# Storing the stream in token order from a ScalarE copy beside layer two, reading it without a step in the scan layer, and a gate product placed behind the eighth scan

## The chip, the core and the metric

The kernel runs on one core of one Trainium2 chip, as one launch. The metric is the device time of that launch in microseconds (us). The kernel before the change took 3594.66 us as the median of 3 runs (3594.13 to 3596.95). Five engines work on one program: PE multiplies matrices into PSUM, DVE and ACT work on vectors, POOL is the general engine, and SP issues most of the transfers. Each has an instruction stream of its own, and they meet at semaphores.

## What is computed

An input of three images, 256 channels, 48 x 48 pixels, runs through four layers, each of which adds its result to the stream and begins with a group norm over 32 groups:

```python
x = x + L0(gn(x))    # 1x1 convolutions, two blocks of attention across the images, MLPs
x = x + L1(gn(x))    # 3x3 convolution whose weights are mixed from 8 experts per image
x = x + L2(gn(x))    # 3x3 convolution
x = x + L3(gn(x))    # a selective scan (Mamba) over the 2304 pixels of each image
...
# L3, for tokens l in order, d of 512 inner channels, n of 16 states:
xn = layernorm(x); x_in, z = split(xn @ in_proj)
u  = silu(causal_conv4(x_in)); dt_raw, B, C = split(u @ x_proj)
dt = softplus(dt_raw @ dt_proj + bias)
h[l] = exp(dt[l] * A) * h[l-1] + dt[l] * B[l] * u[l]
y[l] = sum_n h[l] * C[l] + u[l] * D
out  = (y * silu(z)) @ out_proj
```

Everything is float32. The change touches the end of L2 and all of L3.

## The kernel before, in words

**The stream and its order.** Between the layers the stream of an image lies in SBUF as `xs[b]`, 128 partitions x 2 groups of channels (`ct`) x 2304 pixels. The pixels are in phase order: pixel column modulo 4 is the outer index `j`, so that a Winograd transform of the 3x3 convolutions reads and writes packed rows. The scan layer needs the pixels as tokens one after the other.

**Layers one and two** are one loop over `halves` (L1442): six units (two layers x images 2, 1, 0, the tuple `ORDER`), each in an upper and a lower half `h`. For each half, `input_transform` (L295) of the *next* half is emitted first: ACT writes the normalised pixels, padded, into the one buffer `xpad`, and twelve DVE operations make `vt` from it (`L329` and `L334` are the last that read `xpad`, in one or the other order). Then `output` (L1364) runs twice, for m = 0 and 1: six groups of six matmuls each (`products`, L1352) go to one of five PSUM banks `ps_c`; ACT copies every second one to `cb` (L1372), and DVE adds sums and differences to `xs[b]`; the last two go straight from PSUM to `xs[b]` (L1386). After a unit, `next_norm` (L1413) takes the moments of the finished image with two ACT passes over it (`moments`, L1393, which writes its waste into `xpad`). In layer two, after the lower half, six DMAs per image store `xs[b]` to the DRAM tensor `xd[b]` (L1460), chunk by chunk, with the phases still outermost within a chunk: runs of 96 elements. SP issues them, ACT those of the last image.

**Preparation beside layer two.** The generator `early_preparation` (L1272) is advanced after each group of `products` from unit 4 on: it loads chunks 0 and 1 of the stream, normalises them and does the scan layer's projections for chunk 0. A scheduler in the layer below decides the final order of instructions of each engine in this stretch from estimated times; in the attention and in the scan layer the order is the one written out (`keep_order`, L1660).

**The scan layer** goes over 18 chunks of 384 tokens (six per image). A chunk has 8 steps (m of 4 groups of inner channels, h of 2 groups of states). A step is eight scans on DVE (`scan`, L1569), each fed by a decay that ACT computes into one of three PSUM slots (`decay`, L1556), so that ACT can be three ahead. Then DVE and POOL fill the next step's buffer (`fill`, L1529), POOL multiplies the states by C (`times_c`, L1576), and PE sums over the states into `ps_y` (`add_states`, L1585, of the step before). `gate` (L1602) multiplies the finished sum of a group m by silu(z); it is called in the second step of the next group, after scan 6 (`part == 5`, L1625), and it frees the single `ps_y` bank for the next group's first product, D times u (L1592). Three lists of stages (`plan`, `after`, `gating`, L1217 to L1264) place the preparation of the next chunks and the output of the last one into the steps; the place MID is after scans 2 and 6, LATE after 4 and 8, PE_ on PE's stream. Among them:

- `group_scale` (L1053): reads the loaded chunk `xp`, applies the group norm and writes it to `xg` in token order, a step of four elements on the write side; then `less_mean`, `centre`, `square_mean`, `inverse_root`, `normalise` and `tokens` make the layer norm.
- `silu` (L1122): a table load, a Silu over 1536 elements, a table load back, once for u (after m = 1, h = 1) and once for z (after m = 0, h = 0).
- `residual` (L1204) loads the chunk again into `ot`; `project_y` (L1196) multiplies by out_proj and adds the residual with a matmul by the identity (L1202), which reads `ot` through `in_order` (L1049): every step along the tokens is 96 elements. `store` (L1208) copies to `ot` and sends it out.
- `spread` (L1497) loads `dtr` and `dtur`, dt and dt times u, from DRAM for each m. SP's DMAs take turns on eight semaphores, and a DMA waits for the one that used its semaphore before.

Of the kernel before, what the change touches and what calls it, by code (L numbers as in the profile page):

```python
# [9 lines left out]
F32 = mybir.dt.float32  # L10
I32 = mybir.dt.int32
AF = mybir.ActivationFunctionType
# [4 lines left out]
P = 128  # L17
B = 3
HW = 48
N = HW * HW  # L20
CT = 2
# [4 lines left out]
CH = 384  # L26
NCH = N // CH
# [56 lines left out]
def net(  # L84
# [66 lines left out]

    ycat = [dram.tile([P, 3, N], F32, name=f"ycat{b}", bufs=1) for b in range(B)]

    xd = [dram.tile([P, NCH, CT, CH], F32, name=f"xd{b}", bufs=1) for b in range(B)]
    norm3 = {}

    def rsqrt_eps(var, n):
# [67 lines left out]
    def exp_ln_tables():  # L225

        nc.scalar.preload_act_table_set("natural_log_exp_and_others")
# [715 lines left out]


    psg = ctx.enter_context(tc.tile_pool(name="psg", bufs=1, space=PSUM))
    rooms, w3v, chunks = {}, {}, {}

    def room(k, name):
        return rooms[name][k.at % len(rooms[name])]
# [15 lines left out]
    def w3_rooms():  # L965

        block = upools[0].tile([P, 6, 3, CT, 256], F32, name="u")
        block = block.rearrange("p a b c d -> p (a b c d)")
        w3v.update(divide(
            block, ("w3sb", P, (NW3,)), ("wtap", P, (DCONV, CT, DI * P)), ("dtsb", DTR + 1, (DI * P,)),  # L970
            ("amat", P, (DI * DS,)), ("rep", P, (4, 32)), ("less", P, (2, P)), ("zero", P, (8,)),
            ("xn0", P, (CT, CH + DCONV - 1)), ("xn1", P, (CT, CH + DCONV - 1)),
        ))
        rooms["xn"] = [w3v["xn0"], w3v["xn1"]]
        pieces = [wst.tile([P, 3 * 256], F32, name="wconv") for _ in range(6)]
        halves = [t.rearrange("p (t n) -> p t n", t=2) for t in pieces]
        for name, got in zip(("xp", "xg", "sq", "ot"), (halves[:1], halves[1:2], halves[2:3], halves[3:5])):
            rooms[name] = got
        rooms["dbc"] = [halves[5][:96, j, :] for j in range(2)]

# [52 lines left out]
    def fetch(at):  # L1033
        k = chunks[at] = Chunk()
        k.at = at
        k.b, k.c = todo[at]
        k.before = chunks.get(at - 1)
        k.xp = room(k, "xp")
        nc.sync.dma_start(k.xp, xd[k.b][:, k.c])

    class Chunk:
        pass
# [3 lines left out]

    def in_order(t):  # L1049

        return t.rearrange("p (j n) -> p n j", j=4)

    def group_scale(k):  # L1053
        sc, sh = norm3[k.b]
        k.xg = room(k, "xg")
        for ct in range(CT):
            nc.scalar.activation(
                k.xg[:, ct, :].rearrange("p (n j) -> p j n", j=4),
                k.xp[:, ct, :].rearrange("p (j n) -> p j n", j=4), AF.Identity,
                bias=sh[:, ct : ct + 1], scale=sc[:, ct : ct + 1],  # L1060
            )

# [133 lines left out]
    def project_y(k, mo):  # L1196
        for m in range(DI):
            nc.tensor.matmul(  # L1198
                bank[mo], w("out", m * 256 + mo * P, P), k.sz[:, m, :],
                start=m == 0, stop=False,  # L1200
            )
        nc.tensor.matmul(bank[mo], ident, in_order(k.ot[:, mo, :]), start=False, stop=True)  # L1202

    def residual(k):  # L1204
        k.ot = room(k, "ot")
        nc.sync.dma_start(k.ot, xd[k.b][:, k.c])

    def store(k, mo):  # L1208
        nc.scalar.copy(k.ot[:, mo, :], bank[mo])  # L1209
# [56 lines left out]
    def run(at, j, place):  # L1266
        for when, where, rel, stage in after + plan + gating:
            if (when, where) == (j, place) and 0 <= at + rel < len(todo):
                stage(chunks[at + rel])


    def early_preparation():  # L1272

        exp_ln_tables()
        fetch(0)
        winx, cwb = x2_rooms()
        k = chunks[0]
        yield
        while 2 not in norm3:
            yield  # L1280
        group_scale(k)
        yield
        for tap in (0, 1):
            fold_taps(winx, cwb, tap)
        less_mean(k)
        yield
        centre(k)
        yield
        square_mean(k)
        yield  # L1290
        for tap in (2, 3):
            fold_taps(winx, cwb, tap)
        inverse_root(k)
        yield
        normalise(k)
        tokens(k)
        fetch(1)
        yield
        for m in (0, 1):
            taps(k, m, 0, 4)  # L1300
            yield
        take_u(k, 0)
        take_u(k, 1)
        yield
        for m in (2, 3):
            taps(k, m, 0, 4)
            yield
        take_u(k, 2)
        take_u(k, 3)
        silu(k.u)  # L1310
        yield
        k = chunks[1]
        for stage in (group_scale, less_mean, centre, square_mean, inverse_root, normalise):
            stage(k)
            yield
        tokens(k)
        yield

        k = chunks[0]
        while 1 not in norm3:  # L1320
            yield
        x1_rooms()
        yield
        project_u(k)
        yield
        take_dbc(k)
        yield
        for m in (0, 2):
            project_dt(k, m)
            yield  # L1330
            softplus(k, m)
            yield
            take_dt(k, m)
            yield
            keep_dt(k, m)
            yield
        for m in (0, 2):
            for j in range(2):
                project_z(k, m + j, j)
            yield  # L1340
            for j in range(2):
                take_z(k, m + j, j)
            yield


    with ExitStack() as l1:
# [88 lines left out]
        def between():  # L1435
            next(pending, None)
            if at_unit >= 4:
                next(early, None)

        vt = first_v  # L1440
        pending = iter(())
        for n, (k, h) in enumerate(halves):  # L1442
            layer, b = units[k]
            at_unit = k
            if k == 3 and h == 0:
                w3_rooms()
                w3_loads()
            ahead = transformed(n + 1) if n + 1 < len(halves) else None
            u = weights[B if layer else b]
            for m in range(2):  # L1450
                output(b, h, m, u, vt, v("l2_bias", 0, 2) if layer else None)
                for _ in range(13):
                    next(beside.get(k, iter(())), None)
            vt = ahead
            if layer and h == 1:
                phases = xs[b].rearrange("p t (j n) -> p (t j) n", j=4)

                queue = nc.sync if k + 1 < len(units) else nc.scalar
                for c in range(NCH):
                    queue.dma_start(  # L1460
                        xd[b][:, c].rearrange("p t (j n) -> p (t j) n", j=4),
                        phases[:, :, c * (CH // 4) : (c + 1) * (CH // 4)],
                    )
            if h == 1:
                for _ in pending:
                    pass
                pending = next_norm(layer, b)
                next(pending)
        for _ in pending:
            pass  # L1470
        for _ in early:
# [8 lines left out]
    with ExitStack() as l3:  # L1480
# [121 lines left out]
        def gate(at, m):  # L1602
            k = chunks[at]
            nc.vector.tensor_tensor(k.sz[:, m, :], k.y_ps[:, :CH], k.sz[:, m, :], ALU.mult)
# [10 lines left out]
        for s, (at, m, h) in enumerate(steps):  # L1615
            if m == 0 and h == 1 and at + 2 <= last:
                fetch(at + 2)
            for part in range(8):
                j = 4 * m + 2 * h + part // 4
                scan(s, part)  # L1620
                decay(8 * s + part + 3)
                if part == 4 and s + 1 < len(steps):
                    first_states(s + 1)
                if part % 4 == 1:
                    if h == 1 and part == 5 and s >= 3:  # L1625
                        gate(*steps[s - 3][:2])
                    run(at, j, MID)
                if part % 4 == 3:
                    run(at, j, LATE)
                if part == 3:  # L1630
                    run(at, j, PE_)
                    if s + 1 < len(steps) and h == 0:
                        more = [(at, m + 1)] if m + 1 < DI else [(at + 1, 0)]
                        for c, n in more:
                            if c <= last:
                                rows = getattr(chunks[c], "rows", {})
                                chunks[c].rows = {**rows, n: spread(chunks[c], n)}
            if s + 1 < len(steps):
                fill(s + 1)
            last_states(s)  # L1640
            times_c(s)
            run(at, 4 * m + 2 * h + 1, PE_)
            if s >= 1:
                add_states(s - 1)

            if h == 0 and s + 2 < len(steps):
                spread_pe(chunks[steps[s + 2][0]], steps[s + 2][1])
# [122 lines left out]
```

## Time and profile before

| | |
|---|---|
| median of 3 runs | 3594.66 us |
| the profiled execution, its own time | 3598.05 us |
| its span, first to last instruction | 3596.3 us |
| busy: PE, DVE, ACT, POOL | 3179.0, 3003.0, 2333.6, 1440.4 us |
| mean granted clock of PE | 0.934 of full speed |
| layer two | about 1846 to 2098 us |
| first scan, last gate | 2107.6 us, 3581.7 us |

In the views that follow, a row of groups gives the line, the engine, the operation, output<-input and shapes, how many there were, then busy us and mean ns of one, then the idle time of the engine just before them and who ended it. A row in order of time gives start and length in us, and in square brackets the idle time before it and who ended it. "128x384" is partitions x elements. Idle time of an engine that is not the bottleneck of its stretch costs nothing. Each slice of the busy tenths is 89.9 us.

### The profile page before, as it was taken

How to read it: one execution, taken by the hardware profiler on the slowest of the kernel's cores; microseconds unless marked ns; L12 is line 12 of the kernel's file. 1: busy time of each engine (PE TensorE's matmuls, PEld its weight loads, DVE VectorE, ACT ScalarE, POOL GpSimd, SP SyncE). 2: the span in 40 equal slices, each digit the busy share in tenths (PEclk: the TensorE clock that was granted, in tenths of full speed). 3: DMA queues.
4: the chain of work that ended last, by engine and by line, in shares of the span. 5: the costliest groups of instructions: out<-in, count | busy, mean ns of one | idle time of the engine just before them, and what ended most of it. 6: DMA issues, size and time to landing. Idle time of an engine off the chain costs nothing. (4 is left out here: it accounts for less than half of the span.)

```text
span 3596.3 us, 45582 instructions
## 1 busy us (share of the span) xinstructions
PE 3179.0 (88%) x17154; PEld 1438.0 (40%) x17154; DVE 3003.0 (84%) x3304; ACT 2333.6 (65%) x3477; POOL 1440.4 (40%) x386
## 2 busy tenths in 40 slices
PE   7999999999999999977899987888888888788875
PEld 4323232352322324546677743333333333333331
DVE  4798989959989896479965379999999999999996
ACT  2788787748877875332123447777777777777774
POOL 0000000000000000210000059999999999999998
PEclk9999999999999999988999988889999999888986
DMA  4000000000000001756402234444444444444441
GB/s 181 3 1 1 1 2 1 1 40 1 1 1 1 2 1 60 243 171 219 164 28 58 60 75 116 102 112 106 111 98 111 102 108 101 118 106 107 107 106 36
DMA packets 170648, 266.50 MB, mean 74 GB/s; under 512 B 42849, under 2 KB 137633, under 8 KB 168498
## 3 DMA queue, kind: packets, MB, share of 16 engines
q1 hardware_dynamic: 152082, 243.44, 25.2%
q10 hardware_dynamic: 18336, 20.06, 1.7%
q8 instruction: 136, 2.23, 0.3%
q14 instruction: 94, 0.77, 0.1%
HBM read 216.31 MB, written 46.89 MB: 73 GB/s over the span
## 5 line engine op out<-in xcount | busy, mean ns | idle before, releaser
L610 ACT ACTIVATE pt<-ps_s 128x1024 f32<-128x1024 f32 x972 | 939.0, 1022 | 236.9 <-PE ps_s L606 219.3
L1572 DVE TENSOR_TENSOR_SCAN hs<-ps_da,hs 128x385 f32<-128x385 f32 x1152 | 1012.8, 939 | 63.2 <-ACT ps_da L1564 45.4
L686 DVE TENSOR_TENSOR part<-part,pt 128x2048 f32<-128x2048 f32 x396 | 906.5, 2289 | 79.4 <-ACT pt L610 54.8
L1564 ACT ACTIVATE ps_da<-dtr,u 128x384 f32<-128x384 f32 x1152 | 658.0, 582 | 311.1 <-DVE hs L1572 292.6
L162 POOL TENSOR_TENSOR rstd<-ve,mhalf 128x2 f32<-128x2 f32 (+1 forms) x26 | 17.9, 691 | 1529.1 <-DVE ve L160 1529.1
L606 PE MATMUL ps_s<-q,kt 32*128 32x512 f32 (+1 forms) x4320 | 615.2, 593 | 2.3 <-DVE q L567 0.9
L619 PE MATMUL acc<-pt,vt 128*32 128x512 f32 (+1 forms) x4320 | 522.3, 562 | 8.1 <-DVE o L666 8.0
L1356 PE MATMUL ps_c<-vt,u 128*128 128x288 f32 x1728 | 430.0, 410 | 45.7 <-DVE u L261 45.7
L1580 POOL TENSOR_TENSOR hc<-hs,x 128x3072 f32<-128x3072 f32 x72 | 445.6, 6188 | 37.8 <-PE ps_g L1155 13.4
L1580 POOL TENSOR_TENSOR hc<-hs,bc 128x3072 f32<-128x3072 f32 x72 | 444.1, 6169 | 37.7 <-DVE hs L1572 14.1
L1109 PE MATMUL ps_g<-u 128*128 128x384 f32 x1152 | 389.2, 493 | 3.1 <-ACT u L1118 3.1
L1356 PEld LDWEIGHTS ps_c<-vt,u 128*128 128x128 f32 x1728 | 330.3, 192 | 140.1 <-issue 34.8
L606 PEld LDWEIGHTS ps_s<-q,kt 32*128 32x128 f32 x4320 | 220.0, 183 | 388.5 <-issue 227.1
L1109 PEld LDWEIGHTS ps_g<-u 128*128 128x128 f32 x1152 | 215.0, 190 | 174.5 <-issue 14.0
L1597 PE MATMUL ps_y<-hc,u 128*32 128x384 f32 x2304 | 246.1, 550 | 30.7 <-POOL hc L1580 27.4
L1539 POOL TENSOR_TENSOR hs<-dtur,x 128x1536 f32<-128x1536 f32 x72 | 247.9, 3443 | 17.4 <-DMA dtur<-dtud 8.8
L1539 POOL TENSOR_TENSOR hs<-dtur,bc 128x1536 f32<-128x1536 f32 x72 | 248.5, 3451 | 6.5 <-ACT ps_g L1087 2.4
L619 PEld LDWEIGHTS acc<-pt,vt 128*32 128x32 f32 x4320 | 95.7, 108 | 363.8 <-issue 328.1
L1155 PE MATMUL ps_g<-wconv,u 17*128 17x384 f32 x144 | 79.2, 684 | 97.2 <-ACT x L1176 97.2
L1372 ACT COPY cb<-ps_c 128x288 f32<-128x288 f32 x48 | 19.0, 396 | 219.1 <-PE ps_c L1356 200.7
L1067 PE MATMUL ps_g<-wconv,u 128*128 128x384 f32 x144 | 87.5, 780 | 67.0 <-ACT x L1176 66.6
L1597 PEld LDWEIGHTS ps_y<-hc,u 128*32 128x32 f32 x2304 | 64.6, 118 | 201.9 <-issue 151.0
(236 smaller groups left out, 3517.1 us busy)
## 6 DMA issues: line engine op xcount, KB each, us to landing
wconv<-in_we SPq DMA_DIRECT2D x144, 384.0 KB, 4.3
dtr<-dtd SPq DMA_DIRECT2D x288, 192.0 KB, 3.8
dtur<-dtud SPq DMA_DIRECT2D x288, 96.0 KB, 4.1
wconv<-xd SPq DMA_DIRECT2D x36, 384.0 KB, 4.4
x<-bcd SPq DMA_DIRECT2D x72, 192.0 KB, 5.8
dtd<-x SPq DMA_DIRECT2D x36, 384.0 KB, 2.4
bc<-bcd SPq DMA_DIRECT2D x72, 192.0 KB, 5.5
yc<-ycat ACTq DMA_DIRECT2D x18, 576.0 KB, 4.7
```

Of the source, the lines that this page charges most:

```text
L606: nc.tensor.matmul(s[:, j, cols], kt[r, mt * P : (mt + 1) * P], q[r, :n], start=True, stop=True,)
L610: nc.scalar.activation(p[:, h0 : h0 + 2, :], s, AF.Exp)
L619: nc.tensor.matmul(acc[h * HD : (h + 1) * HD, :n], vt[:, mt, g * P + h * HD : g * P + (h + 1) * HD], p[:, h, cols], start=mt == 0, stop=mt ...
L686: nc.vector.tensor_tensor(part, first_p if group == 1 else part, p, ALU.add)
L1067: nc.tensor.matmul(bank[to], w3v["less"][:, int(to != ct), :], k.xg[:, ct, :], start=ct == 0, stop=ct == CT - 1,)
L1109: nc.tensor.matmul(bank[m % 2], w3v["wtap"][:, tap, ct, m * P : (m + 1) * P], k.xn[:, ct, tap : tap + CH], start=tap == 0 and ct == 0, sto ...
L1356: nc.tensor.matmul(pc[:, :HN], u[:, i, dy, ct, m * P : (m + 1) * P], vt[:, i, ct, dy * TW : dy * TW + HN], start=ct == 0 and dy == 0, stop ...
L1539: nc.gpsimd.tensor_tensor(hs[:, :, 2:4, 1:], k.rows[m][1].unsqueeze(1).broadcast_to([P, 2, 2, CH]), bb, ALU.mult,)
L1564: nc.scalar.activation(slots[n % 3][:, 1 : CH + 1], chunks[at].rows[m][0][:, q, :], AF.Exp, scale=amat[:, col : col + 1],)
L1572: nc.vector.tensor_tensor_scan(b, slots[(8 * s + part) % 3][:, : CH + 1], b, 0.0, ALU.mult, ALU.add)
L1580: nc.gpsimd.tensor_tensor(hc, tiles[s][:, :, :, 1:], cb.broadcast_to([P, 2, 4, CH]), ALU.mult)
L1597: nc.tensor.matmul(k.y_ps[32 * q : 32 * q + 32, :CH], fold, hc[:, g, q, :], start=False, stop=h == 1 and g == 1,)
```

## The change

The stores of layer two no longer read the phases. After each half of a layer-two unit, ACT copies the half to token order (two copies of 128 x 1152, written at a step of four elements) into a buffer, and one DMA stores it. The copy of a half is emitted between the two calls of `output` of the next half. The buffer is the single `xpad`; for the very last half, which has nothing behind it, it is a `vt` buffer, and ACT issues the DMA. `xd[b]` is now channels x tokens. A chunk is loaded straight into one of two `xg` buffers (before: one `xp` and one `xg`), `group_scale` works there in place without a step, and the identity's matmul reads `ot` without a step. `early_preparation` waits, while the program is written, until the halves that it loads from have been stored. The gate is called after scan 8 instead of scan 6.

```diff
-    xd = [dram.tile([P, NCH, CT, CH], F32, name=f"xd{b}", bufs=1) for b in range(B)]
+    xd = [dram.tile([P, CT, N], F32, name=f"xd{b}", bufs=1) for b in range(B)]
...
-        for name, got in zip(("xp", "xg", "sq", "ot"), (halves[:1], halves[1:2], halves[2:3], halves[3:5])):
+        for name, got in zip(("xg", "sq", "ot"), (halves[:2], halves[2:3], halves[3:5])):
...
-        k.xp = room(k, "xp")
-        nc.sync.dma_start(k.xp, xd[k.b][:, k.c])
+        k.xg = room(k, "xg")
+        nc.sync.dma_start(k.xg, xd[k.b][:, :, k.c * CH : (k.c + 1) * CH])
...
     def group_scale(k):
         sc, sh = norm3[k.b]
-        k.xg = room(k, "xg")
         for ct in range(CT):
             nc.scalar.activation(
-                k.xg[:, ct, :].rearrange("p (n j) -> p j n", j=4),
-                k.xp[:, ct, :].rearrange("p (j n) -> p j n", j=4), AF.Identity,
+                k.xg[:, ct, :], k.xg[:, ct, :], AF.Identity,
                 bias=sh[:, ct : ct + 1], scale=sc[:, ct : ct + 1],
             )
...
-        nc.tensor.matmul(bank[mo], ident, in_order(k.ot[:, mo, :]), start=False, stop=True)
+        nc.tensor.matmul(bank[mo], ident, k.ot[:, mo, :], start=False, stop=True)
...
-        nc.sync.dma_start(k.ot, xd[k.b][:, k.c])
+        nc.sync.dma_start(k.ot, xd[k.b][:, :, k.c * CH : (k.c + 1) * CH])
...
         exp_ln_tables()
+        while (2, 1) not in stored:
+            yield
         fetch(0)
...
-        while 1 not in norm3:
+        while 1 not in norm3 or (1, 1) not in stored:
             yield
...
+        def store_tokens(b, h):
+            last = (b, h) == (ORDER[-1], 1)
+            if last:
+                t = vp.tile([P, 6, CT, (HR + 2) * TW], F32, name="vt")
+                t = t.rearrange("p i t n -> p (i t n)")
+            else:
+                t = pad.tile([P, 4, CT * (HR + 2) * PW + 2], F32, name="xpad")
+                t = t.rearrange("p j n -> p (j n)")
+            t = t[:, : CT * 4 * HN].rearrange("p (t n) -> p t n", t=CT)
+            for ct in range(CT):
+                nc.scalar.copy(
+                    t[:, ct, :].rearrange("p (n j) -> p j n", j=4),
+                    xs[b][:, ct, :].rearrange("p (j n) -> p j n", j=4)[
+                        :, :, h * HN : (h + 1) * HN
+                    ],
+                )
+            queue = nc.scalar if last else nc.sync
+            queue.dma_start(xd[b][:, :, h * 4 * HN : (h + 1) * 4 * HN], t)
+            stored.add((b, h))
+
         vt = first_v
-        pending = iter(())
+        behind, pending = None, iter(())
...
+                if m == 0 and behind is not None:
+                    store_tokens(*behind)
+                    behind = None
             vt = ahead
-            if layer and h == 1:
-                phases = xs[b].rearrange("p t (j n) -> p (t j) n", j=4)
-                queue = nc.sync if k + 1 < len(units) else nc.scalar
-                for c in range(NCH):
-                    queue.dma_start(
-                        xd[b][:, c].rearrange("p t (j n) -> p (t j) n", j=4),
-                        phases[:, :, c * (CH // 4) : (c + 1) * (CH // 4)],
-                    )
+            if layer:
+                behind = b, h
...
+        store_tokens(*behind)
...
                 if part % 4 == 1:
-                    if h == 1 and part == 5 and s >= 3:
-                        gate(*steps[s - 3][:2])
                     run(at, j, MID)
+                if h == 1 and part == 7 and s >= 3:
+                    gate(*steps[s - 3][:2])
                 if part % 4 == 3:
                     run(at, j, LATE)
```

More of the change, by code (lines that the diff above doesn't have):

```diff
@@ L945, in net @@
     psg = ctx.enter_context(tc.tile_pool(name="psg", bufs=1, space=PSUM))
-    rooms, w3v, chunks = {}, {}, {}
+    rooms, w3v, chunks, stored = {}, {}, {}, set()
     def room(k, name):
@@ L1045, in net @@
     bank = [psg.tile([P, 512], F32, name=f"ps_g{j}")[:, :CH] for j in range(2)]
-    def in_order(t):
-        return t.rearrange("p (j n) -> p n j", j=4)
     def group_scale(k):
         sc, sh = norm3[k.b]
-        k.xg = room(k, "xg")
         for ct in range(CT):
             nc.scalar.activation(
-                k.xg[:, ct, :].rearrange("p (n j) -> p j n", j=4),
-                k.xp[:, ct, :].rearrange("p (j n) -> p j n", j=4), AF.Identity,
+                k.xg[:, ct, :], k.xg[:, ct, :], AF.Identity,
                 bias=sh[:, ct : ct + 1], scale=sc[:, ct : ct + 1],
```

## The prediction, made before the changed kernel ran

> **What bounds the kernel now.** I read the busy tenths first, then who waited for whom in the scan layer, then one chunk of that layer in order of time, then the groups by shape, last the chain that ended last.
>
> ```profile
> span 3596.3 us, 45582 instructions
> ...
> PE   7999999999999999977899987888888888788875
> DVE  4798989959989896479965379999999999999996
> ACT  2788787748877875332123447777777777777774
> POOL 0000000000000000210000059999999999999998
> ```
>
> The change touches two stretches. Layer two, 1846 to 2098 us (slices 21 to 24), is bound by PE: the table by stretches gives PE 99.6 of 100 us from 1850 to 1950 and 100 of 100 from 1950 to 2050, with ACT at 30 and 35 of 100. The scan layer, 2107 to 3582 us, is bound by DVE: 1359 busy of 1475 us. POOL is close behind (1377, though its spans are rough), so I must see that it doesn't take over. DVE's waits there, from 2200 to 3570 us (us in total, times, longest):
>
> ```profile
> DVE hs L1572 <- ACT ps_da L1564: 38.5, 48, 1.0
> DVE wconv L1091 <- ACT ps_g L1087: 17.8, 15, 1.3
> DVE x L1604 <- PE ps_y L1597: 11.3, 16, 1.1
> DVE sz L1604 <- PE ps_y L1597: 11.3, 16, 1.1
> ```
>
> The gate's product (L1604) makes 22.6 us of the 78.9. The whole trace has 33.3: the missing 10.8 is the last gate, which nothing follows. One chunk in order of time, around the gate of m = 1:
>
> ```profile
> 2629.13 5.21 DVE L1572 TENSOR_TENSOR_SCAN hs<-ps_da,hs 128x385 f32<-128x385 f32 x6
> 2635.39 0.56 DVE L1604 TENSOR_TENSOR x<-ps_y,x 128x384 f32<-128x384 f32 x1 [1.05 <-PE ps_y L1597]
> 2635.87 1.80 DVE L1572 TENSOR_TENSOR_SCAN hs<-ps_da,hs 128x385 f32<-128x385 f32 x2
> 2637.58 1.73 DVE L1535 TENSOR_TENSOR hs<-ps_r,x 128x1536 f32<-128x1536 f32 x1
> 2639.42 2.66 DVE L1572 TENSOR_TENSOR_SCAN hs<-ps_da,hs 128x385 f32<-128x385 f32 x3
> 2643.12 4.36 DVE L1572 TENSOR_TENSOR_SCAN hs<-ps_da,hs 128x385 f32<-128x385 f32 x5 [1.04 <-ACT ps_da L1564]
> ```
>
> Six scans, a wait of 1.05 us for PE, the gate, two scans, the fill, three scans, and a wait of 1.04 us: ACT has three decays ready and then spends 1.28 + 1.48 + 1.28 us on a table load, the Silu of u and a table load back. Each chunk of about 82 us holds two gate waits (m = 0: 0.36, m = 1: 1.05), two Silu waits, and 0.30 + 1.17 us around the normalisation.
>
> ```profile
> L1202 PE MATMUL ps_g<-wconv,ident 128*128 128x384 f32 x72 | 52.8, 822 | 0.0
> L1198 PE MATMUL ps_g<-sz,u 128*128 128x384 f32 x144 | 51.0, 498 | 0.0
> L1057 ACT ACTIVATE wconv<-wconv,norm 128x384 f32<-128x384 f32 x36 | 34.3, 1052 | 3.5 <-DVE norm L1425 3.5
> L1101 ACT ACTIVATE u<-wconv,vec 128x384 f32<-128x384 f32 x36 | 23.4, 698 | 2.0 <-DVE wconv L1091 2.0
> ```
>
> The strided matmul (L1202) takes 822 ns beside 498, the strided group_scale (L1057) 1052 beside 698 for the same Identity on packed rows.
>
> [...] L1202 reads at a step of 384 bytes and L1057 writes at 16 bytes[...]
>
> **Scan layer: the gate (-22.6, then -8.0).** It moves behind scan 8, so two scans (1.73 us from start to start) now run in front of it. The longest wait was 1.1 us, so all 32 go: -22.6. What could be late next? The decays of the two scans: at m = 1, ACT had issued the one for scan 7 by 2633.2, and that for scan 8 comes behind the store's copy, which itself waited 0.67 us for L1202 and will be earlier; needed at 2635.2, there at 2634.9 at worst. After the gate stands the fill, which no wait preceded. The WAR on ps_y: PE's diagonal product (L1592) waits for the gate; at m = 2 PE got there at 2658.80 and the gate will end at about 2658.8; at the other three m PE has over 2 us of other work first. POOL's product waits for scan 8, which comes 0.47 us earlier (gate no longer before it).
> A second effect: at m = 1 the Silu of u starts on ACT when scan 8 ends. Today DVE fills that time with 1.73 + 2.56 us, then waits 1.04. The gate now adds its 0.47 us (start to start) of work there. 17 chunks have this Silu: -8.0. The other Silu (after m = 0, h = 0) has no gate in that step and stays.
> POOL per step: 3.45 + 6.18 = 9.63, 77 us per chunk of 82. The chunk becomes 1.41 + 0.47 = 1.88 shorter, 80 us. Laying POOL's 9.63 against the new step ends by hand, POOL falls up to 1.8 us behind DVE in the short steps and catches up in the long ones; its halves of the fill are needed four scans into a step, which leaves over 4 us. No loss.
>
> **Scan layer: packed rows (-1.3).** 36 group_scales save about 0.35 us each, 12.7 us of ACT; but in the chunk shown ACT then idles 0.49 us for DVE, and no scan waits there: 0. If that cover went, 12.7. 72 records of L1202 save 0.32 us, 23 us of PE, all behind the gate wait already counted, but for the end: the chain that ended last holds two pairs of it, 1.31 and 1.32 us, beside 2.58 / 4 = 0.645 for a packed pair: -1.3. The loads of xd take the place of loads as large; group_scale needs them some 30 us after their issue even where the built order puts them behind eight dtur loads on SP's queue. They wait for a normalisation long done, so nothing on SP is held: 0.
>
> **Layer two: the copies (+1.5).** Added: 12 ACT copies of 128x1152. [...] the stride adds (1052 - 698) / 384 = 0.92 ns per element, 1.06 us: 2.2 us each as an estimate, 26 us in all. Bounds: [...]3.2 (three group_scales). Removed: 18 DMA issues in 384-byte runs (12 on SP, 6 on ACT), for 6 in 4608-byte runs.
> Do they reach PE? The copies use the xpad tile, so in the built order ACT waits for the input transform to have read it (DVE L329), copies, and the next writes of xpad wait until SP's store has landed. Behind them on ACT stand the copies of ps_c that free PE's five banks, and the first group_scale. After image 2's last half: xpad is read by 1931.2, copies to 1935.6, store landed some 4.7 later (median of stores today 4.2, the 1152 KB ones 4.2 to 4.9) at 1940.3, two transform writes of 1.34 to 1943.0, the ps_c copy to 1943.4 (today 1940.4), the first group_scale to 1944.1. PE needs that bank at about 1948, no loss. But its less_mean stands three matmuls earlier in the new order: PE arrives at 1942.8 and waits about 1.5 us (0.33 today). A second boundary (image 1) holds ps_c about 3 us, and PE's next need is 4 us later. With what the halves in between may add: +1.5, between 0 and +8; below nothing there is no gain, since PE had no idle time.
>
> **The hand-over (0).** After the last ps_c (2098.3) ACT had 3.70 us of DMA issues; now 2.2 of copy and one issue. The first decay waits for dtr (2105.7), issued before both. The fourth dtur quarter shares a semaphore with the last store and waits for it: landed at 2105.5 to 2108, where SP today ended at 2107.3. 0, between -2.5 and +3.
>
> **Sum.** -22.6 - 8.0 - 1.3 + 1.5 = -30.4. The profiled execution took 3598.05 (span 3596.3): 3567.6. The median of the runs is 3594.66, 3.4 lower: 3564.3.
>
> **Rivals.** (a) Half: the freed DVE meets other waits in its chunk (ACT's in-order work, or POOL at 94%), and the second effect fails: about -15, 3580. For it: POOL's margin is 3 us per chunk. Against: DVE waited for POOL for only 1.6 us in this layer. 16%. (b) More: dtr lands 2.5 us sooner without the 384-byte stores beside it, and shorter ACT and PE work also trims the 0.30 + 1.17 and the Silu waits: -42, 3553. 8%. (c) Slower: in layer two each store holds ACT for copies and landing, 2 x 2.2 + 4.7 = 9.1 us, and PE runs dry: five stores inside the layer, +45, with -31.9 elsewhere: 3608. PE's five banks last 5 x 2.91 = 14.5 us; the longest gap between two ps_c copies comes to about 15.3 us by the above. It ends slower once PE loses over 38 us, 7.7 per store. Against: banks are freed in the order of use, and I find one place of 1.5. 7%. (d) No change: stores cost PE some 30 us, or the 22.6 reappears at the Silu: 3593. 7%. The likeliest, 62%, has its own range 3556 to 3573.
>
> Within 0.2% (7 us) is about what a measurement here can't tell from no change. Faster 0.86 (likeliest, a, b), same 0.07, slower 0.07. The range, with (a) and (b) in: 3550 to 3584.
>
> **What would show it.** After: no waits of L1604 for PE but the last; Silu waits of about 0.5 and 1.04 us in turn; the ident matmul near 500 ns and group_scale near 700; twelve copies of about 2.2 us; PE idle by some 1 to 2 us ahead of the first less_mean. Wrong if the copies take 3 us or more and PE idles in layer two, or if scans wait for POOL.

## The result and the profile after

The changed kernel takes 3560.45 us (median of 4 runs, 3559.11 to 3564.10) beside 3594.39 us for the kernel before: a ratio of 0.9907, 95% interval 0.9889 to 0.9924. That is 33.9 us less by the medians; forecast were 30.4 less, 3564.3. The profiled execution took 3559.81 us with a span of 3558.1.

First the busy tenths of the changed kernel:

```profile
span 3558.1 us, 45649 instructions
...
PE   7999999999999999977899987878888888878875
...
DVE  4798989959989897379975469999999999999997
ACT  3788787848887876332123447777777777777774
POOL 0000000000000000210000029999999999999998
```

Nothing has changed sides: PE still fills layer two, DVE the scan layer. Next who DVE waited for in the scan layer (2160 to 3530 us; us in total, times, longest):

```profile
DVE hs L1587 <- ACT ps_da L1579: 30.5, 43, 1.0
DVE wconv L1085 <- ACT ps_g L1081: 16.4, 15, 1.3
```

Both rows of the gate (now L1619) are gone. The row behind decays fell from 38.5 to 30.5; over the whole layer the 17 waits behind the Silu of u make 8 us of that (17.1 and 9.2), and those behind the Silu of z stayed at 18.4. The same place in a chunk, around the gate of m = 1, in order of time:

```profile
2623.00 0.53 DVE L1619 TENSOR_TENSOR x<-ps_y,x 128x384 f32<-128x384 f32 x1
2623.45 1.75 DVE L1550 TENSOR_TENSOR hs<-ps_r,x 128x1536 f32<-128x1536 f32 x1
2625.30 2.66 DVE L1587 TENSOR_TENSOR_SCAN hs<-ps_da,hs 128x385 f32<-128x385 f32 x3
2628.53 4.36 DVE L1587 TENSOR_TENSOR_SCAN hs<-ps_da,hs 128x385 f32<-128x385 f32 x5 [0.57 <-ACT ps_da L1579]
```

The gate follows scan 8 with no wait, the fill follows the gate, and the wait behind the Silu of u is 0.57 us where it was 1.04. The groups that the change made cheaper or new:

```profile
L1196 PE MATMUL ps_g<-wconv,ident 128*128 128x384 f32 x72 | 29.1, 486 | 0.0
L1052 ACT ACTIVATE wconv<-wconv,norm 128x384 f32<-128x384 f32 x36 | 23.3, 693 | 1.8 <-DVE norm L1421 1.8
L1448 ACT COPY xpad<-x 128x1152 f32<-128x1152 f32 x10 | 22.4, 2328 | 13.0 <-DVE we L329 5.6 <-DMA xd<-xpad 5.4 <-DVE vt L334 1.9
```

In layer two PE now loses time in one place, here in order of time, PE, then ACT, then DVE:

```profile
1938.36 3.64 PE L1352 MATMUL ps_c<-vt,u 128*128 128x288 f32 x14
1945.20 2.85 PE L1061 MATMUL ps_g<-wconv,u 128*128 128x384 f32 x8 [3.20 <-ACT wconv L1052]
```

```profile
1939.71 2.67 ACT L310 ACTIVATE xpad<-x,six 128x1200 f32<-128x1200 f32 x2 [5.83 <-DMA xd<-xpad]
...
1944.44 1.30 ACT L1052 ACTIVATE wconv<-wconv,norm 128x384 f32<-128x384 f32 x2 [1.78 <-DVE norm L1421]
```

```profile
1943.03 1.23 DVE L1014 TENSOR_TENSOR u<-x 128x1024 f32<-128x1024 f32 x1 [1.62 <-DMA x<-in_convw]
1944.17 0.16 DVE L1420 COPY norm<-gsc 128x2 f32<-128x2 f32 x1
1944.24 0.16 DVE L1421 COPY norm<-gsh 128x2 f32<-128x2 f32 x1
```

ACT waits 5.83 us until the store has left `xpad`, transforms the next half and makes one copy of `ps_c`, to 1942.66 us. Then it waits again, 1.78 us, for the scale and shift of the group norm (`norm`) from DVE, and this wait ended last. DVE had the operands since about 1941.4, but the two copies of `norm` stand behind a product (L1014, it folds the convolution's taps into weights) that waited 1.62 us for the convolution's weights. SP issued that load from 1935.19 us on, behind the store of 1933.90; in the kernel before it issued it at 1923.43. The weights go into the room of image 2's stream, so they can't come before that stream has been copied out.

**Where the time went**, from marks that both traces have. The span fell by 38.2 us: the stretch up to layer two -1.2 (the norm matmul at 1796.29 and 1795.11 us, which the change can't reach); layer two +2.3 (from there to the end of the last `ps_c`: 301.56 and 303.89); the hand-over to the first scan -2.1 (9.78 and 7.66); the scan layer from first scan to last gate -36.4 (1474.1 and 1437.7); the tail -0.9 (14.6 and 13.7). About 4 us of the 38.2 is that the profiled execution of the kernel before was 3.7 above its median and that of the changed kernel 0.6 below; which stretch that belongs to, one profile doesn't tell.

### The profile page after: what moved, and what is told of

It reads as the page before. It is cut to its first block, busy times and chain, and to the rows that moved or that the text cites. A ratio compares the mean times of both kernels' runs of the same rounds, so it can differ in the third digit from the quotient of the medians.

```text
span 3558.1 us, 45649 instructions
## 1 busy us (share of the span) xinstructions
PE 3149.5 (89%) x17154; PEld 1435.9 (40%) x17154; DVE 2998.5 (84%) x3304; ACT 2346.8 (66%) x3489; POOL 1439.3 (40%) x386
## 5 line engine op out<-in xcount | busy, mean ns | idle before, releaser
L1595 POOL TENSOR_TENSOR hc<-hs,bc 128x3072 f32<-128x3072 f32 x72 | 444.0, 6166 | 18.9 <-DVE hs L1587 18.2
L1612 PE MATMUL ps_y<-hc,u 128*32 128x384 f32 x2304 | 246.6, 551 | 20.9 <-POOL hc L1595 17.4
L1554 POOL TENSOR_TENSOR hs<-dtur,x 128x1536 f32<-128x1536 f32 x72 | 247.9, 3443 | 17.1 <-DMA dtur<-dtud 11.2
```

Of the source, the lines that this page charges most:

```text
L1554: nc.gpsimd.tensor_tensor(hs[:, :, 2:4, 1:], k.rows[m][1].unsqueeze(1).broadcast_to([P, 2, 2, CH]), bb, ALU.mult,)
L1595: nc.gpsimd.tensor_tensor(hc, tiles[s][:, :, :, 1:], cb.broadcast_to([P, 2, 4, CH]), ALU.mult)
L1612: nc.tensor.matmul(k.y_ps[32 * q : 32 * q + 32, :CH], fold, hc[:, g, q, :], start=False, stop=h == 1 and g == 1,)
```

## The experiments

Two theories. Mine: the gate's place makes the gain, through its own waits and through the Silu of u, and the rows without a step matter in the tail alone. The rival: the stepped reads were holding the layer up, and the rows are a good part of the gain. For every run below I took the same ledger: the time from the start of the first scan to the start of the last gate, all DVE waits inside it, and the remainder. The wait ahead of the first scan belongs to the hand-over and is not in it.

| kernel | median us | ratio to before (95%) | first scan to last gate | DVE waits in it | remainder |
|---|---|---|---|---|---|
| before | 3594.39 | 1 | 1474.1 | 98.2 | 1375.9 |
| changed | 3560.45 | 0.9907 (0.9889 to 0.9924) | 1437.7 | 65.9 | 1371.8 |
| gate_only | 3569.89 | 0.9925 (0.9912 to 0.9939) | 1445.6 | 71.3 | 1374.2 |
| rows_only | 3589.57 | 0.9982 (0.9975 to 0.9989) | 1465.3 | 89.8 | 1375.5 |
| gate_7th | 3570.02 | 0.9932 (0.9918 to 0.9945) | 1448.6 | 75.1 | 1373.5 |
| ident_stepped | 3570.64 | 0.9931 (0.9918 to 0.9945) | 1446.5 | 72.0 | 1374.5 |
| gate_store_later | 3560.37 | 0.9899 (0.9884 to 0.9915) | 1434.9 | 61.2 | 1373.7 |
| copies_twice | 3570.95 | 0.9927 (0.9914 to 0.9941) | 1437.6 | 65.8 | 1371.9 |
| less_mean_later | 3561.39 | 0.9900 (0.9885 to 0.9915) | 1440.0 | 67.8 | 1372.2 |
| after_again | 3561.51 | 0.9904 (0.9888 to 0.9919) | 1438.1 | 66.1 | 1372.0 |
| silu_z_gate | 3556.64 | 0.9890 (0.9873 to 0.9906) | 1430.5 | 55.3 | 1375.1 |
| norm_later | 3558.98 | 0.9897 (0.9880 to 0.9913) | 1435.4 | 63.6 | 1371.8 |
| best | 3557.25 | 0.9896 (0.9879 to 0.9912) | 1436.0 | 64.4 | 1371.6 |
| moves_only | 3559.27 | 0.9895 (0.9879 to 0.9912) | 1436.3 | 62.5 | 1373.8 |

The remainder stays between 1371.6 and 1375.9 us while the layer's time moves by 44: in this layer the time follows the sum of DVE's waits. (The last gate's 11 us are in each sum. The kernel before ran at 3596.4 to 3596.8 beside gate_only and all runs below it, so these are best compared by their ratios or with after_again.)

**gate_only.** The kernel before with this alone:

```diff
-                    if h == 1 and part == 5 and s >= 3:
-                        gate(*steps[s - 3][:2])
                     run(at, j, MID)
+                if h == 1 and part == 7 and s >= 3:
+                    gate(*steps[s - 3][:2])
```

> The kernel before with the gate alone moved behind scan 8; stores, loads and the identity's matmul as before. Theory (the gate's place is the gain: its 22.6 us of waits go, the wait behind the Silu of u falls from 1.04 to about 0.57 us in 17 chunks[...]): 3556 to 3564 us, no wait of the gate for PE but the last, Silu waits 30 to 31 us in total. Rival (the rows without a step carry a good part: with an identity matmul of 0.82 us, PE's sum would still be late at m = 1): gate waits of some 10 us stay, 3570 or more.

Measured: 0.9925, some 8 us short of my theory and at the edge of the rival's range, and yet the gate waits for PE nowhere but at the end, so the rival's mechanism isn't there. The waits behind the Silu of u fell as expected (17.1 to 9.5 us), but all waits behind decays together only went from 42.3 to 38.4, where the changed kernel has 32.3. Sorted by place they show 16 new ones of 0.21 us (3.4 in all), each at the eighth scan just ahead of the gate of m = 1. DVE and then ACT around one of them:

```profile
2618.59 6.06 DVE L1572 TENSOR_TENSOR_SCAN hs<-ps_da,hs 128x385 f32<-128x385 f32 x7
2624.86 0.96 DVE L1572 TENSOR_TENSOR_SCAN hs<-ps_da,hs 128x385 f32<-128x385 f32 x1 [0.21 <-ACT ps_da L1564]
2625.74 0.53 DVE L1604 TENSOR_TENSOR x<-ps_y,x 128x384 f32<-128x384 f32 x1
```

```profile
2621.42 1.30 ACT L1564 ACTIVATE ps_da<-dtr,u 128x384 f32<-128x384 f32 x2
2623.86 0.48 ACT L1209 COPY wconv<-ps_g 128x384 f32<-128x384 f32 x1 [1.14 <-PE ps_g L1202]
2624.24 0.59 ACT L1564 ACTIVATE ps_da<-dtr,u 128x384 f32<-128x384 f32 x1
```

ACT waits 1.14 us for PE's stepped identity matmul to copy its result out (L1209), and the decay of scan 8 stands behind that copy: it starts 0.38 us after the copy does, at 2624.24 and 2623.86. While the gate stood behind scan 6 and waited 1.05 us there, this was hidden.

**rows_only.** The changed kernel with the gate back in its old place (the diff above, reversed).

> The changed kernel with the gate back behind scan 6. Theory: at m = 1 the gate's wait of 1.05 us shrinks by the two identity matmul pairs that PE runs ahead of the sum, 2 x 0.33 = 0.66 us, in 16 chunks: -10.6; the tail -1.3; layer two +1.5 to +2.3, the hand-over up to -2: about -11, 3581 to 3587 us; the wait of 0.36 at m = 0 stays, that behind the Silu stays 1.04. Rival 1 (rows are worth nothing while the gate stands there): 3592 to 3596. Rival 2 (rows are most of the gain): under 3575.

Measured: 0.9982, -6.5 us. The gate's waits, 2160 to 3530 us:

```profile
DVE x L1619 <- PE ps_y L1612: 6.1, 16, 0.4
DVE sz L1619 <- PE ps_y L1612: 6.0, 16, 0.4
```

12.1 us instead of 22.6: the wait at m = 1 falls from 1.05 to 0.39, by the 0.66 expected, and that at m = 0 stays. Rival 2 falls. The median lies 2.6 us above the expected range (the kernel before ran 2.1 us slower beside it, 3596.50). The layer gained 8.8 us (the gate's waits are 10.5 lower, those behind decays 1.8 higher), the hand-over 2.0; but layer two took 305.5 us where the kernel before took 301.6 and the changed kernel 303.9. Behind PE's wait of 3.15 us at the first less_mean the granted clock was 0.66 of full speed from 1946 to 1950 us (1.00 in the changed kernel), and the eight matmuls there took 4.45 us instead of 2.85.

**gate_7th.** The changed kernel with `part == 6` for `part == 7` in the gate's condition.

> The changed kernel with the gate behind scan 7, one scan earlier. Theory: no gate wait either (one scan, 0.86 us, plus the shorter identity matmuls, against 1.05), but the gate no longer lies in the time of the Silu of u, whose wait goes back from 0.57 to 1.04 us in 17 chunks: 8.0 us slower than the changed kernel[...], 3568 to 3572 us. Rival (the Silu wait shrank because ACT has less work ahead of it): as the changed kernel, 3559 to 3562.

Measured: 3570.02, as the theory has it. No gate wait is listed, and the waits behind decays in 2160 to 3530 us are 39.6 instead of 30.5 us: those behind the Silu of u are back, 17.4 us for 9.2. So the gate has two separate effects, and the second needs it behind scan 8, inside the Silu's time.

**ident_stepped.** The changed kernel, but the identity's matmul reads with a step:

```diff
-        nc.tensor.matmul(bank[mo], ident, k.ot[:, mo, :], start=False, stop=True)
+        nc.tensor.matmul(
+            bank[mo], ident, k.ot[:, mo, :].rearrange("p (j n) -> p n j", j=4),
+            start=False, stop=True,
+        )
```

> The changed kernel, but the identity's matmul reads its moving rows at a step of 96 elements again (so the residual is added in another order of pixels). Theory: the 0.33 us per matmul lies behind work everywhere but in the last chunk: +1.3 us, 3561 to 3563, no gate wait. Rival (the gate depends on the shorter matmul): a wait at m = 1 comes back, 3566 to 3572.

(Here the residual lands on other pixels; the run serves for its time alone.) Measured: 3570.64, 9 to 10 us slower than the changed kernel, not 1.3; and again without a gate wait. The 0.21 us waits at scan 8 are back in 16 chunks (3.4 us), the waits in the layer grow by 6.1 us (72.0 against 65.9), the remainder by 2.7, the tail from 13.7 to 15.3. My theory's price for the rows was wrong by about as much as in gate_only, and both traces show the same new place: the store copy.

**gate_store_later.** If the copy's place is the cause, moving it must do as well as the rows. The kernel before with the gate moved, and:

```diff
-        (6, LATE, -1, lambda k: store(k, 0)),
+        (7, MID, -1, lambda k: store(k, 0)),
```

> The kernel before with the gate behind scan 8 and the first store copy of a chunk moved from behind scan 4 to behind scan 6 of the same step, nothing else. Theory (with the stepped identity matmul ACT's store copy waits for PE, and the decay of scan 8 stands behind it: 16 waits of 0.21 us in the gate-only trace): these 16 waits go, waits behind decays from 41.3 to about 37.5 us, 4 to 5 us less than gate-only, ratio to before 0.9910 to 0.9915. Rival (the stepped rows cost elsewhere, in the group scale or at the normalisation): the 16 waits may go, but the time stays within 2 us of gate-only, 0.9925.

Measured: 0.9899, the time of the changed kernel, with all stepped rows left in. At the same place:

```profile
2613.05 6.91 DVE L1572 TENSOR_TENSOR_SCAN hs<-ps_da,hs 128x385 f32<-128x385 f32 x8
2619.88 0.53 DVE L1604 TENSOR_TENSOR x<-ps_y,x 128x384 f32<-128x384 f32 x1
2620.61 1.76 DVE L1535 TENSOR_TENSOR hs<-ps_r,x 128x1536 f32<-128x1536 f32 x1 [0.20 <-PE ps_r L1513]
```

The 16 waits are gone. PE's lateness shows once more, 0.20 us ahead of the fill, but that lies inside the Silu's time and is given back there (0.28 instead of 0.57). The rival, a cost of the stepped rows elsewhere, falls. It gained more than the 4 to 5 us that I expected, 9.5: the waits in the layer fell from 71.3 to 61.2, of which 3.4 stood at scan 8. Another 1.5 is the difference of what the Silu of u lost and the fill gained. And 3.6 went in the last step of a chunk, at the normalisation and the fourth scan (24.9 in gate_only, 21.4 here, 22.1 in the changed kernel, 25.1 in ident_stepped). Why these waits differ was not tried, so the store copy is shown as the cause of the part at scan 8, and the move of it as enough for the rest.

**copies_twice.** The changed kernel with each copy of layer two made twice, `for ct in (0, 1, 0, 1)`.

> The changed kernel with each token-order copy made twice: ACT is held 4.55 us longer per half. Theory (the banks are freed in the order of use and PE meets ACT in one place only): PE's wait ahead of the first less_mean grows from 3.2 to some 7.7 us, one more place may show, and the first scan moves by up to 4.5: 5 to 14 us slower than the changed kernel, 3565 to 3575. Rival (PE pays for every store what it holds): 6 x 4.55 = 27, 3587. Rival (all hidden): 3560 to 3562.

Measured: 3570.95, 9.4 over after_again. PE's waits in layer two:

```profile
PE ps_g L1061 <- ACT wconv L1052: 4.3, 1, 4.3
PE ps_g L1149 <- ACT wconv L1131: 2.4, 1, 2.4
```

Layer two (from the norm matmul to the last `ps_c`) takes 311.7 instead of 303.8 us. 28 us more on ACT (12 copies of 2.33) cost PE 3.6 us of waiting: 1.1 more at less_mean, and a new wait of 2.4. The other 4.2 are slower matmuls right behind these waits, 5.38 instead of 2.85 us for eight and 13.57 instead of 11.91 for 48: the granted clock was 0.50 from 1946 to 1950 us and from 2058 to 2060.5, and 1.00 in both stretches of the changed kernel. As rows_only has such a stretch with the copies made once, this part isn't shown to come from the copies. Neither "all hidden" nor "each store pays". The slower rival of the prediction needed a loss of 38 us.

**less_mean_later.** The changed kernel with one more `yield` ahead of the first `less_mean(k)` in `early_preparation`.

> The changed kernel with one more step of the generator ahead of the first less_mean, so that PE has six matmuls of layer two (2.9 us) more in front of it. Theory (the 3.2 us of PE's wait there are a loss of layer two): the wait falls to 0.3, the time by 2 to 3 us, 3557.5 to 3559. Rival (PE's work behind it waits later for the same copies, or the preparation ends later): no gain, 3560 to 3563.

Measured: 3561.39 beside 3561.51. The wait of 3.2 us is gone, but a new one of 1.23 stands at a norm matmul (L193, for DVE) 95 us later, and layer two shrinks by 1.2 us only, 303.8 to 302.7. No gain that the runs can tell.

**after_again.** The changed kernel itself.

> The changed kernel once more, beside the others on one chip: ratio to before 0.9907 as first measured, 0.990 to 0.9925.

Measured: 0.9904.

**silu_z_gate.** The changed kernel with the other Silu moved into a step that ends in a gate:

```diff
-        (1, LATE, 0, lambda k: silu(k.sz)),
+        (3, LATE, 0, lambda k: silu(k.sz)),
```

> The changed kernel with the Silu of z one step later (behind the step m = 0, h = 1), so that it too begins in a step that ends in a gate. Theory (the gate fills the time of a Silu that starts when scan 8 ends): this Silu's wait falls from 1.04 to 0.57 us in 17 chunks, -8.0: 3551 to 3555 us, waits behind decays from 33.3 to about 25.3. Rival (what falls is the work of ACT ahead of the Silu of u, not the place of the gate): 3559 to 3563.

Measured: 3556.64, just above the range of the theory and the lowest median of the study, 4.9 under after_again; the intervals of their ratios overlap. The mechanism is there: the waits behind decays in the layer fall from 32.3 to 18.9 us (those behind the Silu of z from 18.4 to 6.2) and the layer from 1437.7 to 1430.5. The Silu of z now waits 0.29 with 0.18 ahead of the fill (for PE, 2.6 us in all), and the remainder is 3 us higher, which these runs don't explain. Layer two took 305.4 us, 1.6 more than in after_again, with a granted clock of 0.59 from 1946 to 1950 us behind the wait at less_mean.

**norm_later.** As the last one, and the normalisation too:

```diff
-        (14, LATE, 2, normalise),
-        (15, MID, 2, tokens),
+        (15, MID, 2, normalise),
+        (15, LATE, 2, tokens),
```

> As the one before, and the normalisation's product moved from behind scan 4 to behind scan 6, the pass into token rows (tokens) from behind scan 6 to behind scan 8. Theory (the gate's case again: DVE meets an operand that another engine makes just then, and two scans more in front of it cover it): the 16.4 us of waits ahead of the normalisation go[...]: -18, 3533 to 3537 us. Rival (tokens, 1.5 us on ACT with two small copies, now stands before the decays at a step's end, and scans wait for those): half or more comes back, 3543 to 3552.

Measured: 3558.98; a miss, above the rival's range too, and by another cause than the rival's. (What -18 holds beside the 16.4 us of waits was the author's estimate.) DVE and ACT at the place:

```profile
2663.97 0.96 DVE L1587 TENSOR_TENSOR_SCAN hs<-ps_da,hs 128x385 f32<-128x385 f32 x1 [1.52 <-ACT ps_da L1579]
2664.84 0.93 DVE L1085 TENSOR_TENSOR wconv<-wconv,ps_g 128x768 f32<-128x768 f32 x1
```

```profile
2661.68 0.56 ACT L1080 ACTIVATE ps_g<-ps_g,epst 128x384 f32<-128x384 f32 x1 [0.57 <-PE ps_g L1068]
2662.27 0.47 ACT L1081 ACTIVATE ps_g<-ps_g 128x384 f32<-128x384 f32 x1
2662.97 0.48 ACT L1188 COPY sz<-ps_g 128x384 f32<-128x384 f32 x1 [0.23 <-PE ps_g L1180]
2663.34 1.60 ACT L1579 ACTIVATE ps_da<-dtr,u 128x384 f32<-128x384 f32 x3
```

The normalisation no longer waits (17.6 us in the changed kernel), but scan 6 does (22.7 us in 16 chunks), because its decay stands on ACT behind the inverse root (L1080, L1081) and a copy that wait for PE. The gate's operand comes from PE; this one comes from the engine that also feeds the scans, and moving the reader by two scans didn't help.

**best.** norm_later with the extra `yield` of less_mean_later.

> As the one before, with the first less_mean one generator step later. It took 1.2 us out of layer two when alone: 3532 to 3537 us, 0 to 1.5 less than the one before; the fastest of these.

Measured: 3557.25; a miss too, and not the fastest, for the reason just shown.

**moves_only.** The kernel before (stepped rows, no copies) with the gate, the store copy, the Silu of z, the normalisation and tokens moved as above.

> The kernel before (stepped rows, stores in phase order, no copies in layer two) with moves in the scan layer alone: gate behind scan 8, first store copy behind scan 6, Silu of z one step later, normalisation and tokens two scans later. Theory (once the store copy stands behind scan 6 the stepped rows cost the scan layer nothing, and the copies' cost in layer two equals what the earlier dtr gives back): within 3 us of the same moves on the changed kernel, 3532 to 3539 us. Rival (with fewer waits PE's stepped rows and ACT's stepped group scale show): 5 to 12 slower, 3540 to 3547.

Measured: 3559.27, 0.3 from norm_later: the theory's comparison holds, though both missed its numbers with the normalisation. Once the places in the scan layer are right, the rows bring nothing that the runs can tell.

## Why the prediction was right, and where its parts were not

The measured 3560.45 lies in the range and in the likeliest case, 3.9 under the forecast. By its steps:

- **Gate, -22.6**: right. The two rows are gone, and gate_7th and rows_only show the size: with the packed matmul alone 12.1 us of waits are left.
- **Silu of u, -8.0**: right. The 17 waits fell by 7.9, and gate_7th brings them and about 9 us back.
- **Packed rows, -1.3 in the tail, 0 elsewhere**: the sum holds, the reasoning does not. I wrote that what the stepped matmul saves lies "all behind the gate wait already counted", and that the decay of scan 8 is "there at 2634.9 at worst" for 2635.2. That is true with packed rows. With stepped ones the decay is 0.21 us late in 16 chunks, and gate_only and ident_stepped are about 8 and 9 us slower than the changed kernel. So the full gain of the gate needed either the packed matmul or the store copy moved; I credited it to the gate alone, and that the change brought the packed matmul with it is luck. The tail itself measured -0.9.
- **Layer two, +1.5 (0 to +8)**: +2.3. The place was right, the first less_mean, and so was ACT's part: ACT ended the copy of `ps_c` 0.66 us after PE had come to less_mean (1942.66 and 1942.00), forecast 0.6. The wait was 3.2 instead of 1.5 us because of a term that I left out: the group scale waits for `norm` from DVE. The row of L1057 in the prediction shows 3.5 us of that wait, and I went on as if ACT alone set the time. DVE was 1.62 us late with it, for the convolution's weights that load behind the store. Less that, the wait would have been about 1.6 us, an estimate from these two numbers. The copies' 2.2 us each were an estimate. The trace of before gives about as much: packed passes of ACT over 768 and 1536 elements took 843 and 1484 ns (L1082, L1123), halfway 1.16 us for 1152, and the step of 16 bytes adds the forecast's 1.06 (from L1057 and L1101). Measured: 2.33.
- **Hand-over, 0 (-2.5 to +3)**: about -2. All ten traces with copies and token-order stores have 7.6 to 7.9 us from the last `ps_c` to the first scan, the four without (before, gate_only, gate_store_later, moves_only) 9.7 to 9.8. The first decay waits for dtr in both; its last quarter lands 7.6 us after the last `ps_c` in the kernel before and 5.7 after the change. Two things differ there: the stores beside it no longer go in 384-byte runs, and ACT issues the last one at 2101.84 us, behind the loads of dtr, where before it issued three from 2098.38 on, among them. Neither was tried by itself. This was one half of rival (b).
- **Missing in the sum**: the waits of the layer fell by 32.3 us where I counted 30.6 (those behind decays by 10.0, from 42.3 to 32.3, for the 8.0), and the remainder by 4.1, which I had put at nothing.

Of the rivals, (a), half the gain, did not come; but the stall of ACT that it names is what kept the gate alone at -27 (gate_only). PE waiting for the stores (c) is shown in small by copies_twice. POOL did not take over: DVE waited for it 4.2 us in the whole layer, 2.4 before.

Layer two's +2.3 and the hand-over's -2 cancel, and gate_store_later reaches the same time without either. The copies and the new order in DRAM are therefore not needed for this gain: two moves in the order written for the scan layer make it.

## What to carry to other kernels

When a wait is moved off an engine, list what was hidden inside it, on every engine, and by how much: here the 1.05 us that DVE waited at the gate covered a decay that was 0.21 us late behind another copy. Before moving a reader later, look at what else its producer feeds: the gate's operand comes from PE, and its 22.6 us of waits went; in norm_later the producer is ACT, which also makes the scans' decays, and while the normalisation's 17.6 us of waits went, the scan ahead of it waited 22.7. Before data is laid out anew to shorten an operation, try to move the instruction that waits for it. And when a buffer is read for longer than before, ask which loads now start later: here one such load held DVE up by 1.62 us, about half of PE's new wait of 3.2.

## What was not expected of the hardware

- A wait of DVE took a little more than its number: back to back, a gate starts 0.08 us before the scan ahead of it has ended (in gate_store_later 2619.88 against 2613.05 + 6.91), and the fill that waits behind that gate starts 0.20 us, its whole wait, after the gate's end (2620.61 against 2619.88 + 0.53). In keeping with it, the remainder fell by 4.1 us from before to after, with 39 waits fewer (106 and 67): about 0.1 us for each, an estimate.
- The granted clock was below full speed for some us right behind waits of PE in layer two, but not behind each: 0.66 behind 3.15 us in rows_only, 0.59 behind 3.19 in silu_z_gate, 0.50 behind 4.34 and 2.42 in copies_twice; 1.00 behind 3.20 in the changed kernel; and in after_again, with a wait of 3.12, layer two took 303.8 us, as long as in the changed kernel (303.9). The eight matmuls behind the wait at less_mean took 4.45 us in rows_only and 4.37 in silu_z_gate instead of 2.85, and layer two was 1.6 us longer in both.
- A store of 1152 KB in runs of 4608 bytes took 5.3 us from issue to landing beside layer two (median of five, 4.5 to 5.7), and 6.4 us for the last, which ACT issued.
- Counted from the last `ps_c`, the last quarter of dtr landed after 5.7 us instead of 7.6 once the three stores in 384-byte runs were gone from the same moment; which of the two differences named above did it was not tried.
